# Newton steps of row norms moved to GpSimd, and the last FFN half made in one piece, in a two-layer fp32 network

## Chip, cores, metric

The kernel runs on one core of a Trainium2 chip. The metric is the device time of one execution in microseconds (us), as the median of several runs. Engines are named as in the profile: PE is TensorE's matmuls and PEld its weight loads, DVE is VectorE, ACT is ScalarE, POOL is GpSimd, SP is SyncE, which issues most DMAs.

## What is computed

The input `x` is 2 rows of 1024 tokens of 256 features. Two layers run over it; each sublayer adds its input and normalises the sum over the features (no weights). Layer 0 is causal grouped-query attention with rotary embedding (32 query heads, 8 key heads, 8 features each) and an FFN with int8 weights. Layer 1 is the part that the change touches:

```python
def _L1_attn_ref(x, Wq, Wk, Wv, Wa, ba, Wb, bb, Wg, Wo, ...):   # 16 heads of 128
    q = silu(dwconv_causal(x @ Wq)); k = ...; v = ...
    alpha, beta = sigmoid(x @ Wa + ba), sigmoid(x @ Wb + bb)
    # per head, over time:  err = S k - v;  S = alpha * S - beta * err k^T;  o = S q
    o = (o - mean(o)) * rsqrt(var(o) + 1e-05) * ln_w + ln_b      # over the 128 features of a head
    o = o * sigmoid(x @ Wg)
    return o @ Wo
def _L1_ffn_ref(x, ...):                                          # 256 -> 1024 -> 256
    hidden = relu((x @ sign(up_weight).T) * up_scale)
    return (hidden @ sign(down_weight).T) * down_scale * output_scale
x = layernorm(x + L1_attn(x));  x = layernorm(x + L1_ffn(x))
```

## The kernel before

**Units.** Layer 1 is cut into four *halves* `hi` = 0 to 3 (two halves of 512 tokens for each of two batch rows, `HC` = 4 chunks of 128 tokens each) and, within a half, into 8 pairs of heads `s`. A unit `i` is one half and one pair, 32 in all, and runs the recurrence chunk by chunk. `recur(i)` does, for each chunk, the products `pr` (L661), `pw` (L672), `pm` (L684) and `po` (L699, L700), and takes the statistics of `o` into the small tile `om` (`moments`, L641 and L642).

**Finishing a unit.** `finish` (from L565) is issued about one unit later, beside the next unit's work. It works out 1/sqrt of the variances in `om`, normalises `o` by 128x128 tiles, spread over engines by a string (`NORM`: P is GpSimd, D VectorE, A ScalarE; L594 and L597), transposes on TensorE (`pt`, L603), applies weights (L606) and gate (`y`, L607), splits `y` into a rounded high part `yh` (L610) and a low part `yl` (`sub_low`, L882), multiplies by Wo in three products (`pf`, `mm3`, L932 to L934) and adds into the token rows `xtok` (L622). After the last pair of a half (`s == 7`) the rows are complete and `layernorm` (tile `ln`) makes them the input of the FFN; the rows of halves 0 to 2 are stored to `xs` by SyncE (L892). This text calls that place a *join*: near 1150, 1446 and 1745 us for halves 0, 1 and 2. The last unit has no following work to lie beside, so it finishes in two steps, chunks 0 and 1, then chunks 2 and 3.

**The square root.** 1/sqrt is three Newton steps on tiles of a few numbers per partition, after three setup instructions on VectorE (L896 to L898). On VectorE a Newton step is three instructions (L901 to L903); on GpSimd, which is the form that the `om` of all units but the last uses, it is four (L905 to L908). Each instruction needs the one before it.

```python
if eng is None:
    nc.vector.tensor_mul(t, y, y)
    nc.vector.scalar_tensor_tensor(t, t, -0.5, v, ALU.mult, ALU.mult)
    nc.vector.scalar_tensor_tensor(y, t, 1.5, y, ALU.add, ALU.mult)
else:
    eng.tensor_mul(t, y, y)
    eng.tensor_mul(t, t, v)
    eng.tensor_scalar(t, t, -0.5, 1.5, ALU.mult, ALU.add)
    eng.tensor_mul(y, y, t)
```

`layernorm` (L907 to L919) takes two or four chunks: statistics L913 and L914, the square root on VectorE, and one normalise of 128x256 for each chunk on VectorE (L917).

**The last FFN.** `last_ffn` takes pieces of token columns: one piece of 512 columns for each of halves 0, 1, 2, and two pieces of 256 for half 3. A piece transposes its rows (L763), splits them into `sx2h` (L767, ScalarE) and a low part (L882), then for each of 8 blocks `f` of 128 hidden features makes `ph` (four matmuls, L777 and L778), relu on ScalarE into `sda` (L780), a rounding cast (L781) and a subtraction (L882; on GpSimd for odd `f`, but always on VectorE in half 3) and the four matmuls `po` of the block before (L788). The end scales `po` (L794), transposes back (L800), adds into the rows (L802), normalises (`layernorm`, tile `lf`) and stores.

**Order.** `Places` holds generators with due times in slots (a unit is 120 slots) and takes the one that is due first; what they issue to TensorE is chained in that order (`te.link`). So the order on TensorE is set by hand: `AT_FINISH`, `AT_FINISH_LAST` and `AT_HALF` are the slots of the transposes and products of `finish`, and `FFN1_LAST`, `FFN1_TAIL` the pace of the last FFN. On the other engines a scheduler, which simulates the program while it is built, orders instructions; `tc.high_priority()` moves those inside it ahead. Convolutions of later units run beside all this: ScalarE makes `far` (L289), GpSimd adds it to `q`, `k`, `v` (L292).

Of the kernel before, what the change touches and what calls it, by code (L numbers as in the profile page):

```python
# [3 lines left out]

# [11 lines left out]
AF = mybir.ActivationFunctionType  # L16
ALU = mybir.AluOpType
# [3 lines left out]
P = 128  # L21
B, T, E = 2, 1024, 256
# [8 lines left out]
SCALE = DK ** -0.5  # L31
HP = 2
NS = H // HP
HT = 512
HC = HT // P
# [4 lines left out]
EPS = 1e-5  # L40
# [41 lines left out]
NORM, NORM_LAST = 'PDAPDAPD', 'DDADADAA'  # L82
# [5 lines left out]
AT_BLOCKS, BLOCK_STEP = (44, 52, 145), 2.2  # L88
AT_LEVELS = 43, 53, 73, 83, 103, 113, 132, 142
AT_FFN = 24  # L90
AT_FINISH, AT_FINISH_LAST, AT_HALF = (41, 51, 101, 111), (31, 41, 71, 76), ((22, 30, 46), (12, 18, 36))

FFN0, FFN1, FFN1_LAST, FFN1_TAIL = 7.6, 22.0, 27.0, 40.0

# [50 lines left out]
def delta_rule(  # L145
# [13 lines left out]
    nc = tc.nc  # L159
# [49 lines left out]
    ends = cst.tile([P, 3, H, KS - 1], F32, name="ends", tag="ends")  # L209
# [23 lines left out]
    last = B * 2 * NS - 1  # L233
# [333 lines left out]
    def finish(i, o, m, chunks, places):  # L567

        hi, s = place(i)
        if s == 0:  # L570
            halves[hi]["x"] = load_tokens(pools["late"], hi * HC, HC)
        x = halves[hi]["x"]
        if chunks[0] == 0:
            st[i]["wo"] = []
            for part in range(2):
                t = pools["late"].tile([P, HP, E], F32R, name=f"wo{part}", tag=f"wo{part}", bufs=1)
                nc.sync.dma_start(
                    out=t.bitcast(F32),
                    in_=w1d["o", part][s * HP * P : (s + 1) * HP * P, :].rearrange("(h p) e -> p h e", p=P),
                )  # L580
                st[i]["wo"].append(t)
        wo = st[i]["wo"]
        c1, nc_ = chunks[0], len(chunks)
        t1 = slice(c1 * P, (c1 + nc_) * P)
        rs, nb = m[:, :, 2], m[:, :, 3]
        rsqrt(rs, m[:, :, 1], m[:, :, 4], m[:, :, 5], EPS * SCALE * SCALE, nc.gpsimd if i < last else None)
        nc.vector.scalar_tensor_tensor(nb, m[:, :, 0], -1.0, rs, ALU.mult, ALU.mult)
        for c in chunks:
            for h in range(HP):
                n = (c - c1) * HP + h  # L590
                oc, r1 = o[:, c, h, :], rs[:, n : n + 1]
                how = (NORM if i < last else NORM_LAST)[n]
                if how == "A":
                    nc.scalar.activation(oc, oc, AF.Identity, bias=nb[:, n : n + 1], scale=r1)  # L594
                else:
                    eng = nc.gpsimd if how == "P" else nc.vector
                    eng.tensor_scalar(oc, oc, m[:, n, 0:1], r1, ALU.subtract, ALU.mult)  # L597
        ys = []
        for h in range(HP):
            yield places[h]  # L600
            pt = bank(pools["t"], "t", "pt")[:, 0 : nc_ * P]
            for c in chunks:
                te.link(nc.tensor.transpose(pt[:, (c - c1) * P : (c - c1 + 1) * P], o[:, c, h, :], ident))  # L603
            y = half_tile(pools["late"], "y", 1)[:, 0 : nc_ * P]
            with tc.high_priority():
                nc.scalar.activation(pt, pt, AF.Identity, bias=lnb, scale=lnw)  # L606
                nc.vector.scalar_tensor_tensor(y, st[i]["gt", h][:, t1], 1.0, pt, ALU.add, ALU.mult)  # L607
            yh = pools["late"].tile([P, HT], F32R, name="yh", tag="yh", bufs=2)[:, 0 : nc_ * P]
            yl = pools["late"].tile([P, HT], F32R, name="yl", tag="yl", bufs=2)[:, 0 : nc_ * P]
            (nc.gpsimd.tensor_copy if i < last else nc.scalar.copy)(yh, y)  # L610
            sub_low(nc.gpsimd if i < last else nc.vector, yl, y, yh)
            ys.append((yh, yl))
        for c0 in range(0, nc_, 2):
            yield places[2 + c0 // 2]
            pf = bank(pools["t"], "t", "pf").rearrange("p (c e) -> p c e", e=E)
            for c in range(2):
                for h in range(HP):
                    t = slice((c0 + c) * P, (c0 + c + 1) * P)
                    yh, yl = ys[h]
                    mm3(pf[:, c, :], yh[:, t], yl[:, t], wo[0][:, h, :], wo[1][:, h, :], h == 0, h == HP - 1)  # L620
            xc = x[:, c1 + c0 : c1 + c0 + 2, :]
            nc.vector.tensor_add(xc, pf, xc)  # L622
            if s == NS - 1:
                layernorm(gx, x, c1 + c0, 2)
                halves[hi]["done"] = c1 + c0 + 2
        if s == NS - 1 and hi < 2 * B - 1:
            store_tokens(xs, hi * HC, x)

    def recur(i):

        hi, s = place(i)
# [3 lines left out]
        o = pools["late"].tile([P, HC, HP, P], F32, name="o", tag="o")  # L635
        m = pools["late"].tile([P, HC * HP, 6], F32, name="om", tag="om")

        def moments(c):
            for h in range(HP):
                st6 = pools["late"].tile([P, 6], F32, name="ost", tag="ost")  # L640
                nc.vector.bn_stats(st6, o[:, c, h, :])  # L641
                nc.vector.bn_aggr(m[:, c * HP + h, 0:2], st6)  # L642
            part = HC // 2 if i == last else HC
            if c % part == part - 1:
                chunks = range(c + 1 - part, c + 1)
                at = i * UNIT + 3 * GAP * (c + 1) + 3
                lines.add(finish(
                    i, o, m[:, chunks[0] * HP : (c + 1) * HP, :], chunks,
                    AT_HALF[c // part] if i == last else AT_FINISH_LAST if i == last - 1 else AT_FINISH,
                ), at, at if i == last else (i + 1) * UNIT)  # L650

        for c in range(HC):
# [25 lines left out]
            if hi % 2 == 0 or c < HC - 1:  # L678
# [6 lines left out]
                for h in range(HP):  # L685
                    r = slice(h * P, (h + 1) * P)
                    with tc.high_priority():
                        if M is None:
                            made = nc.vector.tensor_copy(Mn[:, r], pm[:, r])
                        else:  # L690
                            made = nc.vector.scalar_tensor_tensor(
                                Mn[:, r], M[:, r], ge[:, s * HP + h, c : c + 1], pm[:, r], ALU.mult, ALU.add
                            )
# [18 lines left out]
    def last_ffn():  # L712
# [8 lines left out]
        for n in range(4):  # L721
            k, c = n // 2, n % 2 * HT
# [14 lines left out]
            [ring("wk0", [P, HT], F32R, x2) for _ in range(2)], [ring("wk1", [P, HT], F32, x2) for _ in range(2)]  # L737
        )]
        ends = 2 * B - 1
        pieces = [(hi, 0, HC) for hi in range(ends)] + [(ends, c, HC // 2) for c in range(0, HC, HC // 2)]  # L740
        for j, (hi, c0, nc_) in enumerate(pieces):
            if j == 1:
                places.append((
                    [ring("k", [P, HT]) for _ in range(2)], [ring("at", [P, HT], F32) for _ in range(2)]
# [4 lines left out]
            if hi == ends:  # L749
                x = halves[hi]["x"]  # L750
# [44 lines left out]
            for n in range(0, nc_, 2):  # L795
                pt = bank(ps_p, "p", "pt").rearrange("p (c e) -> p c e", e=E)
                for i in range(2):
                    for d in range(2):
                        t = slice((n + i) * P, (n + i + 1) * P)
                        te.link(nc.tensor.transpose(pt[:, i, d * P : (d + 1) * P], ys[d][:, t], ident))  # L800
                xc = x[:, c0 + n : c0 + n + 2, :]
                nc.vector.tensor_add(xc, pt, xc)  # L802
                layernorm(gx, x, c0 + n, 2, "lf")
                store_tokens(out, hi * HC + c0 + n, xc)
                yield 0.5

# [56 lines left out]
def tile_two_layers(ctx: ExitStack, tc: tile.TileContext, a, out):  # L863
    nc = tc.nc
# [15 lines left out]
    def sub_low(eng, lo, full, hi):  # L880

        eng.tensor_sub(lo, full, hi)  # L882
# [11 lines left out]
    def rsqrt(y, var, v, t, eps=EPS, eng=None):  # L894

        nc.vector.tensor_scalar(v, var, eps, None, ALU.add)  # L896
        nc.vector.tensor_scalar(t.bitcast(I32), v.bitcast(I32), 1, None, ALU.logical_shift_right)
        nc.vector.tensor_scalar(y.bitcast(I32), t.bitcast(I32), -1, 0x5F3759DF, ALU.mult, ALU.add)  # L898
        for _ in range(3):
# [7 lines that stand above are left out]
                eng.tensor_scalar(t, t, -0.5, 1.5, ALU.mult, ALU.add)  # L907
                eng.tensor_mul(y, y, t)  # L908

    def layernorm(pool, x, t0, n, tag="ln"):  # L910
        m = pool.tile([P, n, 11], F32, name=tag, tag=tag)
        for i in range(n):
            nc.vector.bn_stats(m[:, i, 5:11], x[:, t0 + i, :])  # L913
            nc.vector.bn_aggr(m[:, i, 0:2], m[:, i, 5:11])  # L914
        rsqrt(m[:, :, 2], m[:, :, 1], m[:, :, 3], m[:, :, 4])
        for i in range(n):
            nc.vector.tensor_scalar(  # L917
                x[:, t0 + i, :], x[:, t0 + i, :], m[:, i, 0:1], m[:, i, 2:3], ALU.subtract, ALU.mult
            )  # L919

    def transpose_split(psum, tag, x, hi, lo, n, col):

# [727 lines left out]
```

## Time and profile before

| | |
|---|---|
| median of three runs | 2069.81 us (2068.07, 2069.81, 2072.84) |
| the profiled execution | 2075.78 us |
| its span on the core | 2074.1 us, 1.7 less than its time |
| mean granted clock of TensorE | 0.975 |
| TensorE busy | 1897.8 us (92% of the span) |
| VectorE, ScalarE, GpSimd busy | 72%, 61%, 50% |

The trace is of the profiled execution, 6.0 us above the median. Lines below such as `PE pt L603 <- POOL o L597` say that an instruction that writes `pt` at line 603 waited for GpSimd's instruction on `o` at line 597. A group `x4` is four like instructions one after the other, its duration from the first start to the last end. The granted clock is the share of full speed that TensorE was given in a stretch.

### The profile page before, as it was taken

Reading aid. Unit: us, or ns where it says so; the run is one execution under the profiler, and the core shown is the slowest. Engines: PE = TensorE matmul, PEld = TensorE weight load, DVE = VectorE, ACT = ScalarE, POOL = GpSimd, SP = SyncE. Lnnn points to the kernel's source line nnn. Section 1 sums busy time; section 2 is a strip of 40 time slices with the busy share of each in tenths; the row PEclk is TensorE's granted clock in tenths of the full one; section 3 lists DMA queues with packets and bytes.
Section 4 is the critical chain, followed back from the end, with each engine's and each line's share of the span. In section 5 each row is a group of like instructions: output and inputs, shape, how many; then the busy total and the mean of one; then the engine's idle time right before and its main releaser. Section 6 shows DMA issues by size and latency. Waiting matters only on the chain.

```text
span 2074.1 us, 49172 instructions
## 1 busy us (share of the span) xinstructions
PE 1897.8 (92%) x18657; PEld 1496.0 (72%) x18657; DVE 1493.4 (72%) x3629; ACT 1269.6 (61%) x2731; POOL 1035.4 (50%) x1539
## 2 busy tenths in 40 slices
PE   5898889999998888899999999998999999999896
PEld 3454455555555777788889888887888888888775
DVE  6755666877757896477786887778678678775576
ACT  1365556576755355567667676766677666676532
POOL 4353333331123453566776656666567676565430
PEclk9999999999999998999999999999999999999997
DMA  5563444442132422443443534444434444443010
GB/s 173 173 185 119 148 127 127 144 135 69 52 76 62 120 74 53 126 129 107 120 132 99 157 99 116 116 122 127 112 114 128 122 115 128 108 132 89 21 41 21
DMA packets 312997, 229.16 MB, mean 110 GB/s; under 512 B 139640, under 2 KB 278904, under 8 KB 312760
## 3 DMA queue, kind: packets, MB, share of 16 engines
q1 hardware_dynamic: 299640, 210.73, 35.0%
q10 hardware_dynamic: 9760, 10.83, 1.6%
q0 software_dynamic: 3360, 4.46, 0.9%
q8 instruction: 147, 2.41, 0.5%
q14 instruction: 90, 0.74, 0.1%
HBM read 171.18 MB, written 51.87 MB: 108 GB/s over the span
## 4 chain that ended last, share of the span: by engine, by line
PE 58%; DVE 13%; ACT 6%; DMA 5%; issue 3%; POOL 2%; SPq 1%; ACTq 0%; POOLq 0%; DVEq 0%
PE pp L932 5%; PE pp L934 4%; PE pp L933 4%; PE ps L1306 4%; PE av L1327 4%; PE ps L1237 3%; PE pkq L506 3%; PE pm L684 2%; DVE at L325 2%; PE pw L672 2%; PE pr L661 2%; PE po L700 2%; PE po L699 2%; PE p L476 2%; PE p L469 2%
## 5 line engine op out<-in xcount | busy, mean ns | idle before, releaser
L1246 DVE TENSOR_REDUCE mx<-ps 128x4 f32<-128x1024 f32 (+1 forms) x320 | 344.3, 1111 | 135.2 <-PE ps L1237 91.2
L1310 ACT ACTIVATE es<-ps 128x512 f32<-128x512 f32 (+1 forms) x608 | 314.0, 577 | 130.2 <-PE ps L1306 119.5
L1306 PE MATMUL ps<-qT,kT 128*128 128x512 f32 (+3 forms) x768 | 221.5, 372 | 21.9 <-ACT es L1310 20.6
L1237 PE MATMUL ps<-kT,qT 128*128 128x512 f32 x576 | 198.8, 419 | 27.8 <-DVE mx L1246 18.7
L1306 PEld LDWEIGHTS ps<-qT,kT 128*128 128x128 f32 x768 | 131.4, 191 | 107.9 <-ACT es L1310 61.5
L1237 PEld LDWEIGHTS ps<-kT,qT 128*128 128x128 f32 x576 | 101.0, 189 | 87.8 <-DVE mx L1246 48.1
L289 ACT ACTIVATE far<-pp,cw 128x509 f32<-128x509 f32 x192 | 133.2, 699 | 47.1 <-DVE v L275 20.8
L1327 PE MATMUL av<-es,vaug 128*32 128x512 f32 (+3 forms) x1536 | 159.4, 503 | 0.2 <-POOL es L1313 0.2
L882 POOL TENSOR_TENSOR wfl<-wf,wfh 128x256 fp32r<-128x256 f32 x80 | 58.6, 734 | 191.0 <-ACT wfh L970 163.0
L1313 POOL TENSOR_SCALAR_AFFINE_SELECT es<-es 128x512 f32<-128x512 f32 x128 | 80.4, 638 | 146.3 <-ACT es L1310 146.1
L275 DVE SCALAR_TENSOR_TENSOR k<-pp,cw,k 128x511 f32<-128x511 f32 (+1 forms) x128 | 92.0, 743 | 46.7 <-ACT k L268 25.0
L275 DVE SCALAR_TENSOR_TENSOR q<-pp,cw,q 128x511 f32<-128x511 f32 (+1 forms) x128 | 93.0, 742 | 45.1 <-ACT q L268 22.2
L292 POOL TENSOR_TENSOR q<-q,far 128x509 f32<-128x509 f32 x64 | 69.4, 1087 | 97.4 <-ACT far L289 97.2
L275 DVE SCALAR_TENSOR_TENSOR v<-pp,cw,v 128x511 f32<-128x511 f32 (+1 forms) x128 | 92.3, 739 | 30.7 <-ACT v L268 18.3
L292 POOL TENSOR_TENSOR k<-k,far 128x509 f32<-128x509 f32 x64 | 78.4, 1227 | 56.8 <-ACT far L289 56.4
L516 POOL TENSOR_TENSOR k<-k,dg 128x508 f32<-128x508 f32 x64 | 81.4, 1271 | 37.9 <-PE pkq L506 32.2
L970 ACT CAST wfh<-wf 128x256 fp32r<-128x256 f32 x80 | 32.4, 406 | 108.0 <-DMA wf<-in_w1k 34.6
L700 PE MATMUL po<-wc,at 128*128 128x128 f32 x512 | 96.6, 275 | 0.0
L664 ACT COPY prs<-pr 128x256 f32<-128x256 f32 x128 | 48.8, 381 | 73.0 <-PE pr L661 64.6
L325 DVE TENSOR_TENSOR_SCAN at<-da,d 128x512 f32<-128x512 f32 x64 | 91.0, 1459 | 0.0
L684 PE MATMUL pm<-wc,kc 128*128 128x128 f32 x448 | 77.1, 295 | 13.0 <-ACT wc L675 12.9
L1327 PEld LDWEIGHTS av<-es,vaug 128*32 128x32 f32 x1536 | 39.1, 110 | 68.2 <-issue 53.8
(314 smaller groups left out, 5942.3 us busy)
## 6 DMA issues: line engine op xcount, KB each, us to landing
wk<-w1k SPq DMA_DIRECT2D x64, 256.0 KB
da<-dec SPq DMA_DIRECT2D x64, 256.0 KB
wv<-w1v SPq DMA_DIRECT2D x64, 256.0 KB
wq<-w1q SPq DMA_DIRECT2D x64, 256.0 KB
dg<-dec SPq DMA_DIRECT2D x64, 256.0 KB
wg<-w1g SPq DMA_DIRECT2D x64, 256.0 KB
wo<-w1o SPq DMA_DIRECT2D x64, 256.0 KB
ad<-avs ACTq DMA_DIRECT2D x32, 256.0 KB
```

The lines of the kernel that those rows point to most:

```text
L275: made = nc.vector.scalar_tensor_tensor(acc[:, d:], pp[:, 0 : HT - d], cw[:, n, hd, KS - 1 - d : KS - d], acc[:, d:], ALU.mult, ALU.add)
L289: made = nc.scalar.activation(far[:, w], pp[:, w], AF.Copy, scale=cw[:, n, hd, 0:1])
L292: nc.gpsimd.tensor_add(acc[:, KS - 1 :], acc[:, KS - 1 :], far[:, w])
L325: nc.vector.tensor_tensor_scan(e, dec, d1.rearrange("p c t -> p (c t)"), 0.0, ALU.mult, ALU.add), taps
L684: te.link(nc.tensor.matmul(pm[:, r], lhsT=st[i]["kc", h][:, c, :], rhs=wc[:, r], start=True, stop=True))
L700: te.link(nc.tensor.matmul(po[:, r], lhsT=st[i]["at", h][:, t], rhs=wc[:, r], start=(M is None), stop=True))
L932: te.link(nc.tensor.matmul(out, lhsT=lhi, rhs=rhi, start=k0, stop=False))
L1237: anchor["mm"] = te.link(nc.tensor.matmul(ps[:, j - j0, :].rearrange("p (g k) -> p g k", k=P), lhsT=q_, rhs=kT[:, :, j * P : (j + 1) * P], ...
L1246: nc.vector.tensor_reduce(mx[:, it, j0 // 2, :], ps[:, 0:n, :].rearrange("p j (g k) -> p g j k", k=P), AX.XY, ALU.max)
L1306: te.link(nc.tensor.matmul(ps[:, g - g0, :], lhsT=kT[:, g, jb * P : (jb + 1) * P], rhs=qT[:, i0 : i0 + w], start=True, stop=True,))
L1310: exps.append(nc.scalar.activation(es[:, g0 : g0 + n, 0:w], ps, AF.Exp, scale=D ** -0.5))
L1327: mm = te.link(nc.tensor.matmul(av[ROW * g : ROW * (g + 1), i0 - ih * 512 : 512], lhsT=vaugs[b][:, jb, kv, :], rhs=es[:, g, 0:w], start=(j ...
```

## The change

The GpSimd form of the Newton steps takes the place of VectorE's in the layernorms at the three joins, in the square root of `om` and in the `ln` of the last unit's first two chunks, and in the output layernorms `lf` of halves 0 to 2. The last step of all (`final`: chunks 2 and 3 of the last unit) and the output norm of half 3 stay on VectorE. The normalising, splitting, adding and layernorm of the last step, and the statistics of the last chunk, are issued with priority. `last_ffn` takes half 3 as one piece of 512 columns, and the slots of the last step's transposes and products are earlier.

```diff
-AT_FINISH, AT_FINISH_LAST, AT_HALF = (41, 51, 101, 111), (31, 41, 71, 76), ((22, 30, 46), (12, 18, 36))
+AT_FINISH, AT_FINISH_LAST, AT_HALF = (41, 51, 101, 111), (31, 41, 71, 76), ((22, 30, 46), (10, 14, 23))
...
+        final = i == last and chunks[-1] == HC - 1
+        slow = None if final else nc.gpsimd
+        ahead = tc.high_priority if final else nullcontext
...
-        rsqrt(rs, m[:, :, 1], m[:, :, 4], m[:, :, 5], EPS * SCALE * SCALE, nc.gpsimd if i < last else None)
-        nc.vector.scalar_tensor_tensor(nb, m[:, :, 0], -1.0, rs, ALU.mult, ALU.mult)
-        for c in chunks:
+        with ahead():
+            rsqrt(rs, m[:, :, 1], m[:, :, 4], m[:, :, 5], EPS * SCALE * SCALE, slow)
+            nc.vector.scalar_tensor_tensor(nb, m[:, :, 0], -1.0, rs, ALU.mult, ALU.mult)
+            for c in chunks:
...
-            (nc.gpsimd.tensor_copy if i < last else nc.scalar.copy)(yh, y)
-            sub_low(nc.gpsimd if i < last else nc.vector, yl, y, yh)
+            with ahead():
+                (nc.gpsimd.tensor_copy if i < last else nc.scalar.copy)(yh, y)
+                sub_low(nc.gpsimd if i < last else nc.vector, yl, y, yh)
...
-            nc.vector.tensor_add(xc, pf, xc)
+            with ahead():
+                nc.vector.tensor_add(xc, pf, xc)
+                if s == NS - 1:
+                    layernorm(gx, x, c1 + c0, 2, eng=slow)
             if s == NS - 1:
-                layernorm(gx, x, c1 + c0, 2)
                 halves[hi]["done"] = c1 + c0 + 2
...
-                nc.vector.bn_stats(st6, o[:, c, h, :])
-                nc.vector.bn_aggr(m[:, c * HP + h, 0:2], st6)
+                with tc.high_priority() if i == last and c == HC - 1 else nullcontext():
+                    nc.vector.bn_stats(st6, o[:, c, h, :])
+                    nc.vector.bn_aggr(m[:, c * HP + h, 0:2], st6)
...
-        pieces = [(hi, 0, HC) for hi in range(ends)] + [(ends, c, HC // 2) for c in range(0, HC, HC // 2)]
-        for j, (hi, c0, nc_) in enumerate(pieces):
+        for j, (hi, c0, nc_) in enumerate((hi, 0, HC) for hi in range(2 * B)):
...
-                layernorm(gx, x, c0 + n, 2, "lf")
+                layernorm(gx, x, c0 + n, 2, "lf", None if hi == ends else nc.gpsimd)
...
-    def layernorm(pool, x, t0, n, tag="ln"):
+    def layernorm(pool, x, t0, n, tag="ln", eng=None):
...
-        rsqrt(m[:, :, 2], m[:, :, 1], m[:, :, 3], m[:, :, 4])
+        rsqrt(m[:, :, 2], m[:, :, 1], m[:, :, 3], m[:, :, 4], eng=eng)
```

## The prediction

> **What bounds the kernel now.** I read the page first (busy shares, engines on the chain that ended last), then the busy time by stretch of the last 55 us, then the timelines of GpSimd, TensorE and VectorE where each half of a batch row ends (the joins).
>
> ```profile
> PE 1897.8 (92%) x18657; PEld 1496.0 (72%) x18657; DVE 1493.4 (72%) x3629; ACT 1269.6 (61%) x2731; POOL 1035.4 (50%) x1539
> PE 58%; DVE 13%; ACT 6%; DMA 5%; issue 3%; POOL 2%; SPq 1%; ACTq 0%; POOLq 0%; DVEq 0%
> ```
>
> TensorE bounds the program. VectorE gains nothing by having less to do unless TensorE waits for it, and it does at the end. Columns below: stretch, its length, busy time (instructions) of PE, PEld, DVE, ACT, POOL, then granted clock, DMA share, GB/s.
>
> ```profile
> 2041.00:2049.00 8.00, 2.78 (x19) 2.18 (x19) 6.18 (x37) 0.84 (x2) 0.00 (x0) 0.91 0.00 1
> 2049.00:2058.00 9.00, 7.92 (x32) 6.75 (x33) 3.48 (x10) 2.28 (x5) 0.00 (x0) 0.51 0.08 29
> 2058.00:2065.00 7.00, 6.05 (x38) 4.76 (x37) 3.60 (x10) 2.45 (x6) 0.00 (x0) 1.00 0.01 2
> 2065.00:2075.00 10.00, 0.88 (x4) 0.45 (x4) 4.38 (x19) 0.50 (x2) 0.00 (x0) 0.65 0.08 26
> ```
>
> TensorE waits while VectorE normalises (first row), pays with half a clock (second), and works at full clock only in the third. Its own rows there:
>
> ```profile
> 2049.30 1.22 PE L763 MATMUL pt<-ident,xtok 128*128 128x128 f32 x4 [5.16 <-DVE xtok L917]
> 2051.20 0.58 PE L777 MATMUL ph<-sx2h,sk 128*128 128x256 f32 x1 [0.68 <-ACT sx2h L767]
> ```
>
> **Price of a Newton step.** GpSimd at the first join (start, duration, in us):
>
> ```profile
> 1150.61 0.21 POOL L905 TENSOR_TENSOR om<-om 128x8 f32<-128x8 f32 x1 [1.83 <-DVE ln L898]
> 1150.89 0.21 POOL L906 TENSOR_TENSOR om<-om 128x8 f32<-128x8 f32 x1
> ...
> 1152.66 0.21 POOL L908 TENSOR_TENSOR om<-om 128x8 f32<-128x8 f32 x1
> 1152.82 1.09 POOL L292 TENSOR_TENSOR v<-v,far 128x509 f32<-128x509 f32 x1
> ...
> 1155.07 2.48 POOL L597 TENSOR_SCALAR o<-o,om 128x128 f32<-128x128 f32 x3
> 1157.52 1.08 POOL L292 TENSOR_TENSOR v<-v,far 128x509 f32<-128x509 f32 x1
> ```
>
> Dependent steps start 0.29 apart, but an independent one follows after 0.16 (1152.66 to 1152.82). A moved layernorm is 12 such steps instead of 9 VectorE ones, which start 0.20 apart alone (2068.48 to 2068.68, below) and 0.10 interleaved. With several chains on GpSimd I take 0.16 a step; the bounds are 0.10 and 0.29.
>
> The Trainium skill, "GPSIMD Engine Reference", section 4.1, calls GpSimd about twice as slow on two-input elementwise work. From VectorE's 0.16 that would be an estimated 0.32 a step, against the 0.21 here; with 113 steps on paths that count (89 at the joins, 24 at the end, below), the total would be 18 us worse than mine.
>
> **Joins.** The finished `o` is normalised, three of eight tiles on GpSimd, and transposed on TensorE (L603):
>
> ```profile
> 1157.21 0.73 PE L603 MATMUL pt<-ident,o 128*128 128x128 f32 x4
> ...
> 1453.80 1.08 PE L603 MATMUL pt<-ident,o 128*128 128x128 f32 x3 [7.11 <-POOL o L597]
> ```
>
> At the first join (the third is alike) nothing waits; at the second TensorE already waits 7.11 us for GpSimd. The change puts the 24 steps of two layernorms among the 12 of `om` on GpSimd, ahead of those tiles. First join, GpSimd from 1150.61: 14 steps x 0.16 = 1152.85, a convolution product L292 (1.09), 8 steps = 1155.25, the second L292 (1.09; it stood behind `o` before), 6 steps = 1157.3, then the tiles at 2.48 / 3 each to 1159.8; ScalarE's share of `o`, behind its convolution work, 1160.2. The transposes end 2.6 later; TensorE's next wait of 0.77 takes part of that, leaving 1.9, twice 3.8. Second join: VectorE, free of 18 steps, delivers its convolutions about 1.6 earlier, but GpSimd has 16 + 3 + 17 steps and two products before `o`, done at 1456.4 instead of 1455.4: +1.0. Behind the first join TensorE waits only 1.3 us in all in 1157 to 1215, so the delay stays; after the third about 0.7 of some 7 us of waits in 1810 to 1925 goes. Joins: 3.8 + 1.0 - 0.7 = **+4.1**, between nothing (the third rival) and 11.6 more (28 + 28 + 33 = 89 steps that count, x 0.13 if each took 0.29). On SyncE the store of the normalised rows waits for the normalises and holds the load of the next rows and of gate weights behind it. It left at 1166.33, 1453.55 and 1754.81; a GpSimd chain ending at 1157.3 does not touch the first, makes the second some 2 us later, where the weight load waits until 1466.50 for TensorE anyway, and the third perhaps 2 later, for weights that come a unit ahead: nothing, at most 2 once.
>
> **Output norms of the first two halves** (12 steps in each of four calls) lie beside matmuls with slack. I take -0.3 for VectorE's lighter queue; the bounds are -1.5 and +2.
>
> **The last unit.** VectorE's two chains, `ln` and `om`, interleave at 2020 to 2023; one step is held by a GpSimd subtraction on 128x512:
>
> ```profile
> 2020.38 1.26 DVE L902 SCALAR_TENSOR_TENSOR ln<-ln 128x2 f32<-128x2 f32 x1
> ...
> 2066.13 0.69 DVE L802 TENSOR_TENSOR xtok<-pt,xtok 128x512 f32<-128x512 f32 x1 [1.95 <-PE pt L800]
> ...
> 2068.48 0.16 DVE L901 TENSOR_TENSOR lf<-lf 128x2 f32<-128x2 f32 x1
> 2068.68 0.16 DVE L902 SCALAR_TENSOR_TENSOR lf<-lf 128x2 f32<-128x2 f32 x1
> ...
> 2070.26 0.73 DVE L917 TENSOR_SCALAR xtok<-xtok,lf 128x256 f32<-128x256 f32 x2
> ```
>
> In the build the whole last FFN stands behind the last finish on TensorE, where before a 256-column piece stood before it. The finish no longer competes with that piece, and priority puts its norm first. Step by step: VectorE is held by the subtraction until 2021.7, then does the Newton steps of the last `om` alone (9 x 0.20) to 2023.5; the first two chunks' `ln`, now a lone chain on GpSimd (10 steps x 0.29), is through at 2024.65, its transposes at 2026.6; those of `o` for the first head at 2027.75, `y` at 2030.1 behind the third half's statistics, the second head's `yl` at 2033.25, the 12 matmuls of `pf` at 2035.1 (2044.0 before). But VectorE's queue has the four normalises of the third half ahead of the add into `xtok` (L622), and they wait for GpSimd's 24 `lf` steps from 2031.1: 24 x 0.16 = 2035.0, normalises to 2036.7, add and layernorm (4.17 from the end of the add, as 2066.82 to 2070.99) to 2041.55, transposes, copy and subtraction as before: first `ph` 2043.2 instead of 2051.20, **-8.0**. At 0.29 a step it would be 3 less.
>
> The FFN is then 64 matmuls of 512 columns for 64 of 256. From the rows before, one takes 0.23 at full clock and 0.43 at half. After the wait TensorE is at half clock; the stretches at half clock in this trace last 3.4 or 10.2 us, and I take 5.1 of this FFN (3.4 to 6.8). Later each of eight blocks costs 1.9. From first `ph` to the scaling of the last `po` comes to 18.2, against 13.46 (2051.20 to 2064.66): **+4.7**. The output stage (ScalarE 1.27 instead of 0.84, two adds of 0.69, four statistics, two interleaved chains of 2.4, four normalises 1.38) is 8.9 against 6.33: **+2.6**. The end: -8.0 + 4.7 + 2.6 - 0.3 = **-1.0**, the -0.3 being that of the output norms.
>
> The clock rows are 0.91 while TensorE waits, then 0.51 for 9 us. The Trainium skill, "TensorE: Matmul & The Clock Gate", Part 1, says a gate halves the clock after an idle window of about 3.4 us and needs about 3.4 us of work to open. That speaks against a change that takes away the matmuls beside the last finish; by it, the half clock would be 3.4 us, 0.9 less than my sum, an estimate. [...]
>
> **Sum.** +4.1 - 1.0 = +3.1. The profiled run took 2075.78 (span 2074.1 and 1.7 around it), 6.0 over the median of 2069.81. On its clock I get 2078.9; on the median's, 2069.81 + 3.1 = **2073.0**. From no change the measurement tells about 0.2%, 4.1 us: faster is below 2065.7, slower above 2073.95.
>
> **Rivals.**
> - *GpSimd's small steps do not overlap* (slower). If a step costs 0.21 even beside other chains, the joins cost 28 x 0.05 twice and 33 x 0.05, the end 24 x 0.05: 5.7 more, **2078.7**; at 0.29 up to 2087. For it: no row shows three chains on GpSimd, and steps beside VectorE's casts stretch to 0.46. Against: the 0.16 above. It decides from 0.17 a step on.
> - *The joins hide it and the last piece runs at full clock* (faster). The delay of `o` passes under queued projections, TensorE makes up at the second join (-1), the last FFN is not cold (-2.6, half of 5.1): -1.0 - 2.6 - 1.0 = -4.6, **2065.2**. It needs the wait before the last `ph` to fall under 3.4 us; I have 5.
> - *Joins hidden, the end as forecast*: -1.0, **2068.8**. Against: 1.3 us of waits in 58.
>
> **How the numbers follow.** Forecast 0.50 (own range 2069.5 to 2077; faster 0.03, same 0.28, slower 0.19), first rival 0.22 (slower 0.21, same 0.01), second 0.16 (faster 0.12, same 0.03, slower 0.01), third 0.12 (faster 0.03, same 0.08, slower 0.01): faster 0.18, same 0.40, slower 0.42. Range 2063.5 to 2081.5: from below the second rival to above the first, without the 0.29 end.
>
> **What would show it.** Right: TensorE waits 2 to 3 us before the transposes of `o` at the first and third join, about 8 at the second; the third half's normalises end just before the add into `xtok`; first `ph` of the last half about 8 us earlier; that FFN 18 us long with 5 cold; 9 us from its end to the store. Wrong: no wait at the joins (third rival), GpSimd steps 0.21 or more apart where chains interleave (first), a granted clock of 1.00 from the first `ph` (second), or the last add not held by the `lf` steps.

## The result and the profile after

The changed kernel takes 2074.07 us in the median of 20 runs (2067.63 to 2078.95), against 2068.30 of the kernel before (20 runs, 2062.54 to 2073.27). The ratio is 1.0023, with a 95% interval of 1.0015 to 1.0032: 3 to 7 us slower. The profiled run took 2074.56 us, close to its median; the profiled run of before lay 6 us above its own (all that comes ahead of the first `wc`, which the change does not touch, took 3.5 us longer in it than in the changed kernel's). So the two spans must not be subtracted. Below, stretches are compared that start and end at the same instruction.

The page of the changed kernel, engines and chain:

```profile
PE 1892.6 (91%) x18593; PEld 1489.7 (72%) x18593; DVE 1479.0 (71%) x3487; ACT 1267.9 (61%) x2721; POOL 1063.2 (51%) x1707
PE 57%; DVE 13%; ACT 6%; DMA 6%; POOL 3%; issue 3%; SPq 1%; ACTq 0%; DVEq 0%; POOLq 0%
```

VectorE lost 14 us of work and GpSimd gained 28. Nothing follows from that, because TensorE still carries the chain. What happened at the first join shows in the timelines, GpSimd first:

```profile
1148.98 0.20 POOL L913 TENSOR_TENSOR ln<-ln 128x2 f32<-128x2 f32 x1
1149.14 0.22 POOL L914 TENSOR_SCALAR om<-om 128x8 f32<-128x8 f32 x1
1149.31 0.20 POOL L914 TENSOR_SCALAR ln<-ln 128x2 f32<-128x2 f32 x1
1149.46 1.09 POOL L292 TENSOR_TENSOR v<-v,far 128x509 f32<-128x509 f32 x1
...
1151.83 1.09 POOL L292 TENSOR_TENSOR v<-v,far 128x509 f32<-128x509 f32 x1
...
1153.86 2.56 POOL L601 TENSOR_SCALAR o<-o,om 128x128 f32<-128x128 f32 x3
```

`om` and `ln` alternate, each step 0.16 after the one before: the price that the sum had taken from a single pair of rows. Both convolution products L292 now stand before the tiles of `o`. TensorE, in the same profile, at the first and second join:

```profile
1154.72 0.33 PE L607 MATMUL pt<-ident,o 128*128 128x128 f32 x1 [0.81 <-POOL o L601]
1156.09 1.13 PE L607 MATMUL pt<-ident,o 128*128 128x128 f32 x3 [1.04 <-ACT o L598]
...
1456.09 1.07 PE L607 MATMUL pt<-ident,o 128*128 128x128 f32 x3 [8.05 <-POOL o L601]
```

Where nothing waited before, TensorE now waits for GpSimd and then for ScalarE, and the 7.11 us of the second join have become 8.05. Behind the first join comes something that the prediction did not have. In the stretches (granted clock third from the end):

```profile
1152.00:1156.00 4.00, 2.24 (x11) 1.59 (x10) 3.96 (x11) 3.43 (x8) 4.00 (x10) 1.00 0.37 87
1156.00:1160.00 4.00, 3.78 (x136) 3.20 (x136) 2.71 (x7) 1.95 (x6) 2.62 (x5) 0.58 0.22 77
1160.00:1164.00 4.00, 4.00 (x152) 3.79 (x153) 2.00 (x6) 4.00 (x13) 3.24 (x9) 1.00 0.04 8
```

TensorE works on through the second row, but at little more than half speed. In the kernel before, the same work (the 128 small products among it) ran at 1.00:

```profile
1158.00:1160.00 2.00, 2.00 (x136) 1.79 (x135) 2.00 (x5) 1.30 (x3) 0.60 (x1) 1.00 0.68 192
```

The end of the program, first GpSimd and VectorE, then TensorE:

```profile
2034.27 0.35 POOL L915 TENSOR_TENSOR lf<-lf 128x2 f32<-128x2 f32 x2
```

```profile
2034.50 1.38 DVE L924 TENSOR_SCALAR sx2l<-sx2l,lf 128x256 f32<-128x256 f32 x4 [1.78 <-POOL lf L915]
2035.80 0.68 DVE L628 TENSOR_TENSOR xtok<-pf,xtok 128x512 f32<-128x512 f32 x1
```

```profile
2040.37 1.23 PE L770 MATMUL pt<-ident,xtok 128*128 128x128 f32 x4 [5.57 <-DVE xtok L924]
2042.27 0.79 PE L784 MATMUL ph<-sx2h,sk 128*128 128x512 f32 x1 [0.67 <-ACT sx2h L774]
```

VectorE stands idle for 1.78 us for the last `lf` step of half 2, does that half's four normalises, and only then the add that the last FFN needs. The first `ph` comes at 2042.27; `ph` of the same rows came at 2051.20 before. The clock, over the wait, the start and the rest of that FFN:

```profile
2033.00:2041.00 8.00, 2.43 (x12) 2.00 (x12) 5.66 (x23) 0.00 (x0) 1.61 (x11) 0.50 0.20 66
2041.00:2048.00 7.00, 6.33 (x17) 4.29 (x16) 2.94 (x6) 1.97 (x3) 0.00 (x0) 0.54 0.00 0
2048.00:2061.00 13.00, 12.54 (x51) 8.65 (x50) 6.78 (x13) 4.13 (x6) 0.00 (x0) 1.00 0.00 0
```

### The profile page after: what moved, and what is told of

Same layout as the page of the kernel before. It is cut to its first block, busy times and chain, and to the rows that moved or that the text cites. A ratio compares the mean times of both kernels' runs of the same rounds, so it can differ in the third digit from the quotient of the medians.

```text
span 2072.8 us, 49051 instructions
## 1 busy us (share of the span) xinstructions
PE 1892.6 (91%) x18593; PEld 1489.7 (72%) x18593; DVE 1479.0 (71%) x3487; ACT 1267.9 (61%) x2721; POOL 1063.2 (51%) x1707
## 4 chain that ended last, share of the span: by engine, by line
PE 57%; DVE 13%; ACT 6%; DMA 6%; POOL 3%; issue 3%; SPq 1%; ACTq 0%; DVEq 0%; POOLq 0%
PE pp L940 5%; PE pp L942 4%; PE pp L941 4%; PE ps L1314 4%; PE av L1335 4%; PE ps L1245 3%; PE pkq L506 3%; PE pm L692 2%; DVE at L325 2%; PE pr L669 2%; PE po L708 2%; PE pw L680 2%; PE po L707 2%; DVE k L275 2%; PE p L476 2%
## 5 line engine op out<-in xcount | busy, mean ns | idle before, releaser
L292 POOL TENSOR_TENSOR q<-q,far 128x509 f32<-128x509 f32 x64 | 69.6, 1089 | 93.2 <-ACT far L289 93.1
L292 POOL TENSOR_TENSOR k<-k,far 128x509 f32<-128x509 f32 x64 | 78.4, 1226 | 57.8 <-ACT far L289 57.3
L692 PE MATMUL pm<-wc,kc 128*128 128x128 f32 x448 | 77.6, 296 | 12.7 <-ACT wc L683 12.6
```

The source lines that it names most:

```text
L292: nc.gpsimd.tensor_add(acc[:, KS - 1 :], acc[:, KS - 1 :], far[:, w])
L692: te.link(nc.tensor.matmul(pm[:, r], lhsT=st[i]["kc", h][:, c, :], rhs=wc[:, r], start=True, stop=True))
```

## The experiments

Times are ratios to the kernel before, run on the same chip in the same batch; e1 to e4, e5 to e8 and e9 to e11 are the three batches. The other columns come from the one profile of each kernel, in us. A *join* column is the stretch from the first copy of `pw` into `wc` in the unit that runs beside the finish (units 9, 17, 25) to the same copy one unit later; the last is from the last such copy of the program to its end.

| kernel | ratio, 95% interval | join 1 | join 2 | join 3 | end |
|---|---|---|---|---|---|
| before | 1 | 39.33 | 48.72 | 42.37 | 61.95 |
| changed | 1.0023 [1.0015, 1.0032] | 42.34 | 50.08 | 42.14 | 60.31 |
| e1_joins | 1.0041 [1.0026, 1.0056] | 43.50 | 48.86 | 41.64 | 61.90 |
| e2_one_piece | 0.9991 [0.9980, 1.0002] | 39.38 | 48.65 | 39.58 | 58.72 |
| e3_no_joins | 0.9999 [0.9986, 1.0011] | 38.81 | 48.73 | 39.80 | 59.68 |
| e4_lf_vector | 1.0021 [1.0006, 1.0036] | 42.60 | 49.27 | 42.40 | 58.88 |
| e5_warm | 0.9978 [0.9964, 0.9992] | 38.77 | 48.89 | 40.00 | 57.73 |
| e6_om_vector | 1.0032 [1.0020, 1.0044] | 45.37 | 46.43 | 45.54 | 60.61 |
| e7_om_vector_only | 1.0035 [1.0021, 1.0049] | 45.95 | 47.16 | 45.82 | 58.15 |
| e8_join_warm | 1.0001 [0.9987, 1.0016] | 41.67 | 47.92 | 40.59 | 59.61 |
| e9_second_join | 0.9944 [0.9926, 0.9963] | 38.72 | 45.57 | 38.75 | 57.70 |
| e10_lf_third | 1.0032 [1.0015, 1.0048] | 43.58 | 49.97 | 41.47 | 59.86 |
| e11_all_warm | 0.9970 [0.9955, 0.9986] | 38.72 | 48.26 | 38.71 | 57.59 |

Single profiles also differ by a wait that no edit aims at. In most join stretches TensorE stands idle once before `p` (L456 to L458) or `px` (L429), and the profile shows nothing that it waits for ("issue"). At the first join this is 0.8 to 2.1 us in the four profiles of the changed kernel, e1, e4 and e10, and 0 to 0.5 in before, e2, e3 and e5; at the third it is 0.6 to 1.6 against 0.7 to 1.9. Its cause is open, and whether the change lengthens it is not shown. Some readings below take it off.

**The joins alone (e1).** The kernel before, and one edit:

```diff
-                layernorm(gx, x, c1 + c0, 2)
+                layernorm(gx, x, c1 + c0, 2, eng=nc.gpsimd if i < last else None)
```

> The kernel before with one part of the change alone: the Newton steps of the six layernorms at the three joins go to GpSimd; the end of the program is as before. Theory (the loss lies at the joins): TensorE waits 1.5 to 2.6 us before the transposes of o at the first and third join (none before) and about 8 us at the second (7.7 in all before); the time is 3 to 5 us above the kernel before. Rival (the joins' waits are made up by queued projections, the loss lies at the end): the waits may show, but the time is within 1 us of before.

TensorE's waits in its first join stretch (us in total, times, longest; first the unexplained one, then those for `o`):

```profile
PE p L458 <- issue: 1.9, 1, 1.9
...
PE pt L603 <- ACT o L594: 1.0, 1, 1.0
PE pt L603 <- POOL o L597: 0.8, 1, 0.8
...
PE pt L603 <- DVE o L597: 0.2, 1, 0.2
```

Those for `o` are 2.0 us, the same three waits as in the changed kernel, and the same again at the third join; 8.6 us at the second. The time is 5 to 12 us above before, even more than expected. The rival, that the joins' waits are made up, is out.

**The end alone (e2), and the change without the joins (e3).**

```diff
# e2, against the changed kernel
-        slow = None if final else nc.gpsimd
+        slow = nc.gpsimd if i < last else None
-                    layernorm(gx, x, c1 + c0, 2, eng=slow)
+                    layernorm(gx, x, c1 + c0, 2)
-                layernorm(gx, x, c0 + n, 2, "lf", None if hi == ends else nc.gpsimd)
+                layernorm(gx, x, c0 + n, 2, "lf")
# e3, against the changed kernel
-                    layernorm(gx, x, c1 + c0, 2, eng=slow)
+                    layernorm(gx, x, c1 + c0, 2, eng=slow if i == last else None)
```

> The changed kernel with all Newton steps where they were before (the norms at the joins, of the last unit's first step and of the output rows on VectorE): only the one-piece last half, the earlier slots and the priority are left. Theory: the joins are as before and the end is a wash: -3 to +0.5 us against before. The first ph of the last half starts 7 to 9 us earlier than in the kernel before, the stretch from it to the last scaling is 18 to 19 us instead of 13.5, the output stage 2.2 to 2.6 us longer. Rival (the longer last piece is what costs): +3 us or more.

> The changed kernel with only the six layernorms at the joins back on VectorE. Theory: no wait before the transposes of o at the first and third join, about 7.7 us at the second; 3 to 5 us below the changed kernel, so 1 to 2 us below before or level with it. Rival (the loss is at the end): level with the changed kernel, 4 to 5 us above before.

The times are as the theory had them. In e2 the first `ph`, counted from the last `wc`, comes 10.4 us earlier than before (7 to 9 expected), the stretch to the last scaling is 18.4, and the output stage is 2.1 longer. Without the joins' part nothing is lost (0.9999), and the one-piece half with its priorities is by itself a small gain or a wash (0.9991, the interval reaches 1.0002). In e2 the waits of the joins are those of the kernel before (none, 7.7, none).

**The output norms (e4, e10).**

```diff
-                layernorm(gx, x, c0 + n, 2, "lf", None if hi == ends else nc.gpsimd)
+                layernorm(gx, x, c0 + n, 2, "lf")                                           # e4
+                layernorm(gx, x, c0 + n, 2, "lf", None if hi >= ends - 1 else nc.gpsimd)    # e10
```

> The changed kernel with only the output norms lf of halves 0 to 2 back on VectorE (18 VectorE instructions for 24 on GpSimd in each half). Theory: within 1.5 us of the changed kernel; at the end the four normalises no longer wait for GpSimd until 2034.5, so the add into xtok comes up to 1 us earlier or later by VectorE's own chains. Rival (the lf steps on GpSimd are what costs): 3 us or more below the changed kernel.

> The changed kernel with only the output norms lf of half 2 back on VectorE. Theory (on VectorE's queue the four normalises of half 2 wait for GpSimd's 24 steps, and the add into xtok stands behind them): the add comes 1 to 1.6 us earlier counted from the last wc, the end likewise; 1 to 1.5 us below the changed kernel, too little for the times alone. Rival (VectorE takes as long for its own 18 steps): the add comes at the same place, 23.3 us after the last wc.

The times cannot tell either kernel from the changed one (the intervals overlap widely). The profile can say where the add into `xtok` stands. In e10, VectorE:

```profile
2034.62 0.69 DVE L628 TENSOR_TENSOR xtok<-pf,xtok 128x512 f32<-128x512 f32 x1 [0.24 <-PE pf L942]
```

That is 22.32 us after the last `wc` (2012.30), against 23.27 in the changed kernel: 0.95 earlier, just under the 1 us expected, and now it waits for TensorE's `pf` and no longer for the normalises. The stretch of the end follows by only 0.45, because the output stage took 0.6 longer in that profile (9.1 from the last scaling to the last normalise, against 8.5). In e4 the add stands 21.63 us after the last `wc`, 1.64 earlier, it too waits for `pf`, and the end is 1.43 shorter. That TensorE's own `pf` is next in line limits what could be had there.

**Extra work against the half clock (e5, e8, e11).** A helper issues matmuls whose result the following transposes overwrite:

```diff
+    def warm(out, lhs, rhs, n):
+        for _ in range(n):
+            te.link(nc.tensor.matmul(out, lhsT=lhs, rhs=rhs, start=True, stop=True))
...
# e5 (on e2), in last_ffn before the transposes of the last two chunks
+                if hi == ends and n == HC - 2:
+                    warm(pt, up[0][:, 0:P], up[0], 12)
# e8 (on the changed kernel), in finish before the transposes of o; e11 (on e5) with (0, 0, 30, 0)
+            if s == 0 and hi > 0 and h == 0:
+                warm(pt, wo[0][:, 0, 0:P], wo[0].rearrange("p h e -> p (h e)"), (0, 8, 30, 8)[hi])
```

> The kernel e2_one_piece with 12 extra matmuls of 512 columns on TensorE ahead of the last transposes of xtok, where it otherwise waits 4.7 us; their result is overwritten. Theory (the last FFN starts at half clock because TensorE stood idle): full clock comes some 3 to 5 us earlier, the stretch from the last transposes to the last scaling falls from 20.3 to 18 to 19 us; 1 to 2.5 us below e2_one_piece. Rival (the blocks' length is set by the chain ScalarE, cast, subtraction and not by the clock): the stretch falls by less than 0.7 us, or the matmuls end late and it grows.

> The changed kernel with extra matmuls of 512 columns, results overwritten, ahead of the transposes of o at the joins: 8, 30 and 8. Theory (behind each wait TensorE runs at half clock for 3.4 us, or 10.2 at the second join, and that doubles the price of the waits): no half clock in 1150 to 1170 and 1445 to 1465; the stretch of the first join shortens by 1 to 2 us, that of the second by 3 to 4; 3 to 6 us below the changed kernel. Rival (the half clock is a matter of where the waits fall and not of TensorE being idle, or the work after it has slack): no change in the stretches beyond 0.5 us.

> The kernel e5_warm and 30 extra matmuls of 512 columns (results overwritten) ahead of the transposes of o at the second join, where TensorE waits 7.7 us. Theory: the half clock of 10 us behind that wait goes, and the stretch of the second join shortens by 1 to 2.5 us; 1 to 2.5 us below e5_warm. Rival (the stretch is set by the wait itself): within 0.5 us of 48.9.

In e5 the clock opens while the extra work runs:

```profile
2034.00:2036.00 2.00, 2.00 (x10) 1.81 (x9) 2.00 (x7) 0.00 (x0) 0.00 (x0) 0.50 0.09 31
2036.00:2038.00 2.00, 2.00 (x7) 1.57 (x6) 1.79 (x10) 0.00 (x0) 0.00 (x0) 0.55 0.70 231
2038.00:2040.00 2.00, 1.31 (x6) 0.74 (x4) 1.73 (x10) 0.00 (x0) 0.00 (x0) 1.00 0.00 0
```

The last FFN then runs at 1.00 from its first matmul, but the stretch from the last transposes to the last scaling falls only from 20.27 to 19.25 (2040.04 to 2059.29): between theory and rival. So the half clock there, 5.4 us of it in e2, cost about 1 us; that ScalarE and VectorE set the rest of the blocks' pace is likely, but was not tried. e5 is the first kernel clearly below the kernel before.

In e8 no half clock is left in any of the three join stretches, and the time comes down to that of before. With the unexplained waits taken off, its first join is 40.9 us against 41.5 in the four profiles with the same waits (changed, e1, e4, e10), the second 47.9 against 48.9 to 50.1, the third 40.6 against 41.5 in the changed kernel, which has half clock there, and 40.8 in the other three, which have none. So the clock was worth about 0.6 at the first join and 0.9 to 2.2 at the second, less than expected. In e11 the ten microseconds of half clock behind the second join go as well, but its stretch falls only to 48.26 from 48.89. It has one of the unexplained waits, which e5 does not have there:

```profile
1461.62 0.99 PE L429 MATMUL px<-n,dt 32*32 32x32 f32 x93 [1.50 <-issue]
```

Without it the stretch would be 46.8, 2.1 below e5, as the theory had it; as it stands the rival is nearer. One profile does not decide this, nor do the times (0.9970 and 0.9978, with intervals that overlap).

**Taking the finished unit off GpSimd (e6, e7, e9).** The same edit on the changed kernel (e6), on e2 (e7), and on e5 for the second join alone, with 20 extra matmuls there (e9):

```diff
+NORM_JOIN = 'DDAADADD'          # NORM is 'PDAPDAPD'
-            rsqrt(rs, m[:, :, 1], m[:, :, 4], m[:, :, 5], EPS * SCALE * SCALE, slow)
+            rsqrt(..., None if s == 0 and hi > 0 else slow)      # with priority; e9: hi == 2
-                    how = (NORM if i < last else NORM_LAST)[n]
+                    how = (NORM_LAST if i == last else NORM_JOIN if s == 0 and hi > 0 else NORM)[n]
```

> The changed kernel with the finished units at the three joins taken off GpSimd: square root of om on VectorE, with priority, and the three GpSimd tiles of o given to VectorE and ScalarE; the layernorms stay on GpSimd. Theory (o waits at the joins because it stands in GpSimd's queue among the moved Newton steps): the waits before the transposes of o at the first and third join fall to 0.5 us or less, that at the second from 8 to under 4; 5 to 9 us below the changed kernel. Rival (o is ready late because VectorE and ScalarE are full at the joins): waits of 1.5 us or more stay at the first and third join, now released by VectorE or ScalarE, and over 5 at the second; within 3 us of the changed kernel.

> The kernel e2_one_piece (all layernorms on VectorE) with the same edit as e6_om_vector: om and all tiles of o at the joins off GpSimd. Theory: no wait at the first and third join, at the second 7.7 falls to under 4 us; 3 to 6 us below e2_one_piece, which makes it the fastest of all so far. Rival (VectorE, with the two layernorms and om, is now late): a wait of over 5 us stays at the second join, released by VectorE, or new waits come at the others; level with e2_one_piece or above.

> The kernel e5_warm, and at the second join alone om on VectorE, its GpSimd tiles of o on VectorE and ScalarE, and 20 extra matmuls of 512 columns (results overwritten) ahead of the transposes of o. Theory: the joins cost waits plus the half clock that follows them, so the stretch of the second join falls from 48.9 to 45 to 46.5 us and the others stay; 2 to 4 us below e5_warm, the fastest of all. Rival (VectorE is late by as much as it was in e7_om_vector_only, and later units lose what the join gains): level with e5_warm.

In e6 and e7 the first and third join got worse: TensorE waits 5.5 and 4.9 us there, for VectorE. VectorE's rows of e7 show why:

```profile
1145.05 0.15 DVE L903 TENSOR_SCALAR om<-om 128x8 f32<-128x8 f32 x1
...
1157.65 0.17 DVE L591 SCALAR_TENSOR_TENSOR om<-om 128x8 f32<-128x8 f32 x1
```

Thirteen instructions of at most 0.17 take 12.6 us, because convolutions of 0.74, the layernorms' chains and other work stand between them on VectorE, with hardly a gap. So the rival holds for these two joins: VectorE is full, and e7 is 9 us slower than e2. It does not make GpSimd innocent, since e1 and e3 differ from their neighbours in nothing but the six layernorms. At the second join, where GpSimd held TensorE already before, the edit gains (47.16 after 48.65). e9 keeps it there alone:

```profile
PE pt L609 <- DVE o L601: 2.2, 1, 2.2
```

Of 7.7 us, 2.2 are left behind the extra matmuls, the stretch is 45.57, and the kernel is at 0.9944 of before: faster than e5 and the fastest of all. By the ratios it is 7 us below e5, where 2 to 4 were expected, but the two intervals leave 2 to 12.

## Why the prediction was right, and where its terms were off

The forecast was 2073.0, +3.1 on the median of before (2069.81, three runs); measured are +4.8 by the ratio. That 2073.0 lies so close to 2074.07 is partly luck: over 20 runs the kernel before is 1.5 us faster than in those three. The direction, the places and the mechanism held; two terms were mis-sized, the joins too small and the end too dear, and cancel in part.

- **Price of a step.** 0.16 was taken, with 0.29 as the bound: the trace shows 0.16 with two and three chains, and 24 `lf` steps from 2030.48 to 2034.5, 0.167 each, two pairs of them slower than the others. The first rival's 0.21 is out. The 0.32 estimated from the Trainium skill ("GPSIMD Engine Reference", section 4.1) does not come out for these small steps: each is busy for 0.20 to 0.21, and with chains that alternate the next one starts after 0.16.
- **Joins, too small.** Forecast +1.9, +1.0, +1.9 and 0.7 back, in all +4.1. Four profiles with the layernorms on GpSimd (changed, e1, e4, e10) have a mean of 43.0, 49.5, 41.9; four with them on VectorE (before, e2, e3, e5) 39.1, 48.7, 40.4: +3.9, +0.8, +1.5, in all +6.2. The waits are as forecast (2.0 of them, and the 0.8 before `px` L429 that the sum set against them is gone). With the unexplained waits taken off, the first and the third join fall into three groups: 38.8 to 39.1 us with the layernorms on VectorE (but 40.5 at the third join of before, which has 3.4 us of half clock); 40.8 with them on GpSimd and the clock full (the third join of e1, e4, e10); 41.5 with them on GpSimd and 3.4 us of half clock (the first join of all four, the third of the changed kernel). So the waits cost 1.9, which is the forecast, and the half clock behind them 0.7 more, which the step "the transposes end 2.6 later" left out; e8 gives 0.6 for it. The Trainium skill, "TensorE: Matmul & The Clock Gate", Part 1, has the clock halved after an idle window of about 3.4 us; here waits of 2.0 us in all were enough, and the measurement decides. Taken so, the three joins cost 4.7 to 5.1 in e1, e4 and e10 and 6.6 in the changed kernel; what is left of the +6.2 is the unexplained waits, less the half clock in before's own third join. Whether the 0.7 is given back later cannot be seen: from there to the last FFN the profiles differ by more than that, with no order.
- **The end, slightly too dear.** Forecast -0.7, and -0.3 for the output norms of the first two halves, which no run measures alone. First `ph` -8.0 forecast; from the last `wc` it is 29.74 against 39.08, so -9.3: the `lf` steps were through at 2034.5, the add began at 2035.80 (forecast: begin after 2036.7). FFN +4.7 forecast, +5.5 measured (18.9 from first `ph` to the last scaling; half clock to about 2047.5, 5.2 us where 5.1 was taken). Output +2.6 forecast, +2.1 measured (2061.18 to 2069.65). Sum -1.7; the table's end column gives -1.6.
- **Second and third rival.** They needed the joins hidden. e1 and e3 rule it out. The full clock in the last FFN, priced at 2.6, was worth 1.0 in e5.

## To carry to other kernels

An engine with idle time is not a free engine: before small dependent steps are moved to it, list what stands behind them in its queue and who waits for that. Here 24 steps of 0.2 us, moved off an engine that was not the bound, stood ahead of three tiles that the bounding engine needed. The reverse move fails in the same way (e7): a chain of short steps in a full queue takes the time of everything between them. And a wait on TensorE of even 2 us in pieces is priced with what its clock does afterwards (0.7 us more here).

## What the runs showed that was not expected

- Waits of 0.8, 0.2 and 1.0 us within 4 us were followed by 3.4 us of half clock at the first join in all four profiles, but at the third join, with the same waits, in one of four. The traces show what differs. In all 13 profiles the clock changes only on a grid of steps of 3.41 us, and the clock of a step goes with how busy TensorE was in the step before. In e1, two steps at the first join and two at the third (the columns are those of the stretches above):

```profile
1154.58:1158.00 3.42, 1.39 (x9) 0.88 (x8) 3.38 (x9) 2.63 (x6) 3.42 (x6) 1.00 0.61 173
1158.00:1161.41 3.41, 3.41 (x136) 3.03 (x135) 2.12 (x5) 2.10 (x6) 1.95 (x4) 0.50 0.02 5
...
1745.09:1748.50 3.41, 1.94 (x10) 1.32 (x9) 3.37 (x9) 2.83 (x6) 3.41 (x10) 1.00 0.35 73
1748.50:1751.92 3.42, 2.89 (x139) 2.49 (x140) 2.85 (x7) 1.33 (x4) 2.16 (x4) 1.00 0.36 119
```

At the first join the waits fall into one step (TensorE busy 1.39 of 3.42 us), at the third they are split over two. Over all 13 profiles, from the first `wc` on: of the steps at full clock, all 37 with TensorE busy for less than 43% were followed by half clock and none of the 4387 with 63% or more; between the two it went either way.
- The way back needs a step nearly full of work: half clock was followed by full clock after all 49 steps busy for 97% or more, and after 1 of 77 below 80%. So through the whole last finish, from about 2023 to 2047, the changed kernel's TensorE was granted half speed, although it was busy for 13.2 of these 24 us: the seven steps were busy for 64, 43, 68, 28, 9, 80 and 100%. In e5 the `pf` products and the 12 extra matmuls, nearly unbroken from 2032 (5.1 us busy in 5.5), brought the clock back to 1.00 before 2038.
- Half a clock can cost less than half of its length: 3.4 us of it at a join about 0.7 us, five in the last FFN about 1.0 (e5). What sets the pace instead was not tried.
